# First layer norm at the end of a group's first half, column tails in one chunk, norm sums on GpSimd, query norm as the exponential's scale

## The chip, the cores and the metric

The kernel runs on one core of one Trainium2 chip. The metric is the device time of one execution in microseconds (us); less is better. The engines of a core work side by side, each through its own queue in order: TensorE (PE, with its weight loads shown as PEld), VectorE (DVE), ScalarE (ACT), GpSimd (POOL) and SyncE (SP), which here only issues transfers. Matmul results land in PSUM banks[...].

## What is computed

Everything is float32. There are 32 sequences of 256 tokens with 256 features. A conditioning attention with 16 heads of 16 features comes first, and then two layers of local attention (8 heads of 64 features, windows of 128 tokens that look at themselves and the window before) and a gated feed-forward with 682 hidden columns. What the change touches is in the layer:

```python
q = l2norm(q) * qs
k = l2norm(k) * ksc
q, k = rotary_xpos(q, k)
o = local_attention(q, k, v)
...
x = x + o @ wo
h = shift_token(x)
mu = h.mean(-1, keepdims=True)
var = h.var(-1, keepdims=True)
h = (h - mu) / jnp.sqrt(var + 1e-05) * lg + lb
h = h @ w1 + b1
a, g = jnp.split(h, 2, axis=-1)
h = a * jax.nn.gelu(g, approximate=False)
x = x + h @ w2 + b2
```

`shift_token` takes the upper half of the features from the token before. The local attention is a softmax over masked scores of q (times 8) and k.

## The kernel before

**Groups and lanes.** Two sequences form a group (G = 2), 16 groups in all. The stream of a group stands transposed in SBUF, features on partitions: `res[:, c, b, 1 + s]` holds feature half c of sequence b. The first column is zero, so the shifted input is a view that starts one column earlier for c = 1. The work of a group is cut into two lanes written as Python generators. `front(p)` (L829) holds, for both sequences, `largest` (maxima of the conditioning scores, L404 to L417), `attended` (their exponentials and weighed sums, L441 to L496), `conditioned`, and then `attention(0)`. `back(p)` (L844) holds `feedforward(0)`, `attention(1)`, `feedforward(1)`, `finish` (output) and `prepare(p + 2)` (the transposes and projections that `largest` of a later group needs). Stage p weaves `front(p)` with `back(p - 1)`. Stage 0 has a front only, and after stage 15 comes one with a back only.

**The order.** Each generator yields before a unit of work, with its kind (THIN or DENSE), a cost in us of TensorE and a delay that has to pass before it may run. `woven` (L859) runs a plan in Python: it takes the lane that is behind, in proportion to the totals FRONT and BACK (L856), and prefers a dense unit when lately there were mostly thin ones. These numbers choose only the order in which instructions are written down. The tile framework then adds the waits, and places instructions of each engine by its own estimate, so that an engine's final order may differ a little from the text.

**The feed-forward** (L714) begins with the layer norm. Two matmuls (one for each feature half) with a 128x128 tile of 1/256, `mean_w`, give the mean of every token on all partitions (L720). VectorE subtracts it (L723), ScalarE squares (L726), and eight matmuls with one column each sum the squares over the features (L732). VectorE adds the epsilon (L740), GpSimd raises to -0.5 (L741), four transposes spread the result over the partitions (L745), and VectorE writes the normalised tile `hl` (L750). The bias `lb` is folded into `b1` at the start (L270). The 682 hidden columns are NJ = 6 chunks of 128, the last with 42 columns. Each chunk of the gate and each of the value is two matmuls with 512 moving columns (L759). Gates go through GELU on ScalarE (L775), values are added and multiplied on VectorE (L783). After three chunks of each, the product with `w2` (L791) is added to the stream.

**The attention** (L514). `projections(t)` for four tiles of 128 tokens makes q, k and v (L535). For q and k, ScalarE squares (L546), VectorE sums over each head (L547) and multiplies with the rotary factors (L550, L555), and GpSimd adds the two rotary parts (L561). At the end GpSimd raises the 16 sums to -0.5 in one instruction (L564) and multiplies q and k by them (L571). `turns` transposes q and k (L586). Then eight items (two heads of one sequence) pass three steps, each a step behind the other. `scores` makes two score tiles (L599), masks them and takes the negative maxima (L614), takes exponentials (L626) and normalises (L639). `turned` transposes the weights (L647) and copies them out of PSUM. `weighed` multiplies by v (L662). `summed` applies the output projection (L676) and adds to the stream (L683). `evacuate` (L111) sends its copies in turn to VectorE (L114) and ScalarE (L116).

**Buffers.** PSUM has four banks `sc`, three `mm` and one `av`. SBUF tiles come from pools: `sb2` (12 buffers of 2 KB), `sb4` (13 of 4 KB), `sb15` (8), and small ones.

## Time and profile before

| what | value |
|---|---|
| time, median of 3 runs | 4487.06 us (4482.97 to 4487.80) |
| the profiled execution: time, span | 4488.3 us, 4486.5 us |
| mean granted TensorE clock | 0.925 |
| L759, feed-forward chunks | 1536 records, 746.8 us busy |
| L535, projections to q, k, v | 1536 records, 720.1 us |
| L732, one-column sums of squares | 512 records, 90.8 us |
| L720, means | 128 records, 66.5 us |
| L626, exponentials of the local attention | 1024, 453.3 us |
| L564, power over 128x16 on GpSimd | 128, mean 2935 ns |
| L741, power over 128x4 on GpSimd | 32, mean 1007 ns |
| L561 and L571, 128x512 on GpSimd | 256 each, mean 1270 and 1055 ns |

A float32 matmul shows as two records on TensorE. Busy times of TensorE are modelled, and records overlap, so the price of one matmul is best read from a long row of equal ones: the time from the first to the last, divided by their number. "Clock" is the share of full TensorE speed that was granted. A busy engine at half clock looks as busy as one at full clock, so both columns have to be read together. A line of a wait names the waiting instruction first, and then the one that released it.

### The profile page before, as it was taken

The numbers are of one execution on the slowest core, as the hardware profiler recorded it, in microseconds if no ns is written. First come the engines' busy times: TensorE is split into PE (matmuls) and PEld (weight loads), VectorE is DVE, ScalarE is ACT, GpSimd is POOL, SyncE is SP. The second block draws the span as 40 slices with busy tenths as digits, with TensorE's granted clock in tenths as the row PEclk, the third lists the DMA queues.
The fourth block names the chain that finished last, engine by engine and source line by source line (L and its number), as shares of the span: only waits on it lengthen the run. The fifth ranks groups of instructions, "written<-read, shape, count | busy, mean of one in ns | idle before, by whom it ended". The sixth has DMA issues, their size and how long they took to land. (4 is left out here: it accounts for less than half of the span.)

```text
span 4486.5 us, 58044 instructions
## 1 busy us (share of the span) xinstructions
PE 4288.5 (96%) x21176; PEld 2460.0 (55%) x21176; DVE 2322.7 (52%) x6679; ACT 1656.2 (37%) x4202; POOL 1079.7 (24%) x840
## 2 busy tenths in 40 slices
PE   7999999999999999999999999999999999999998
PEld 6555645555465555645556455554655556455544
DVE  2347455474644636446374454745447364463734
ACT  0334243342433424244242443424334243342423
POOL 0305040140502305032050411405023050320502
PEclk6889899898998989999898998989989899898999
DMA  3000000000000000000000000000000000000000
GB/s 122 10 1 15 15 11 15 6 15 15 15 15 1 15 15 15 15 1 15 15 15 15 11 13 8 15 15 10 19 2 15 15 15 15 2 15 15 6 5 10
DMA packets 73451, 65.53 MB, mean 15 GB/s; under 512 B 18012, under 2 KB 72016, under 8 KB 73168
## 3 DMA queue, kind: packets, MB, share of 16 engines
q1 hardware_dynamic: 64464, 53.45, 4.3%
q10 hardware_dynamic: 8704, 8.39, 0.5%
q8 instruction: 168, 2.75, 0.3%
q14 instruction: 115, 0.94, 0.1%
HBM read 35.58 MB, written 8.39 MB: 10 GB/s over the span
## 5 line engine op out<-in xcount | busy, mean ns | idle before, releaser
L759 PE MATMUL mm<-t,w 128*128 128x512 f32 (+1 forms) x1536 | 746.8, 628 | 1.7 <-DVE t L750 1.7
L535 PE MATMUL mm<-wqkv,stream 128*128 128x512 f32 x1536 | 720.1, 603 | 0.0
L626 ACT ACTIVATE e<-e,nmf 128x128 f32<-128x128 f32 (+1 forms) x1024 | 453.3, 444 | 407.9 <-DVE nmf L614 407.9
L759 PEld LDWEIGHTS mm<-t,w 128*128 128x128 f32 (+1 forms) x1536 | 269.4, 187 | 388.0 <-issue 368.2
L741 POOL TENSOR_TENSOR rstd<-rstd,minus_half 128x4 f32<-128x4 f32 x32 | 32.2, 1007 | 1832.9 <-DVE rstd L740 1832.9
L561 POOL TENSOR_TENSOR t<-t,t 128x512 f32<-128x512 f32 x256 | 324.3, 1270 | 601.4 <-DVE t L555 574.7
L783 DVE SCALAR_TENSOR_TENSOR t<-mm,b,t 128x512 f32<-128x512 f32 x192 | 143.9, 750 | 565.5 <-PE mm L759 556.4
L535 PEld LDWEIGHTS mm<-wqkv,stream 128*128 128x128 f32 x1536 | 270.8, 190 | 287.4 <-issue 255.3
L404 PE MATMUL sc<-kh,qh 17*128 17x256 f32 x2048 | 372.8, 591 | 11.9 <-DVE mx L412 11.4
L412 DVE TENSOR_REDUCE mx<-sc 128x2 f32<-128x512 f32 x512 | 320.1, 685 | 118.3 <-PE sc L404 117.1
L564 POOL TENSOR_TENSOR ss<-ss,minus_half 128x16 f32<-128x16 f32 x128 | 374.4, 2935 | 4.9
L614 DVE CUSTOM_DVE_ANT_0 e<-sc,misc 128x128 f32<-128x128 f32 (+1 forms) x1024 | 305.1, 351 | 132.9 <-PE sc L599 100.4
L791 PE MATMUL mm<-t,w 128*128 128x512 f32 (+1 forms) x768 | 368.8, 613 | 0.0
L647 PE MATMUL sc<-misc,e 128*128 128x128 f32 x1536 | 269.9, 298 | 86.0 <-DVE e L639 41.6
L451 ACT ACTIVATE t<-sc 128x512 f32<-128x512 f32 x512 | 268.4, 600 | 207.2 <-PE sc L441 133.7
L404 PEld LDWEIGHTS sc<-kh,qh 17*128 17x128 f32 x2048 | 254.4, 268 | 114.1 <-DVE mx L412 72.4
L662 PE MATMUL av<-e,t 128*64 128x256 f32 (+1 forms) x2048 | 306.7, 352 | 0.0
L639 DVE TENSOR_SCALAR e<-e,denf 128x128 f32<-128x128 f32 (+1 forms) x1024 | 292.2, 348 | 3.5
L599 PE MATMUL sc<-t,t 64*128 64x128 f32 (+1 forms) x2048 | 280.5, 365 | 12.9 <-DVE t L114 7.5
L647 PEld LDWEIGHTS sc<-misc,e 128*128 128x128 f32 x1536 | 182.7, 148 | 199.6 <-DVE nmf L614 69.1
L547 DVE TENSOR_REDUCE ss<-t 128x8 f32<-128x512 f32 x256 | 173.5, 678 | 181.0 <-ACT t L546 180.7
L571 POOL TENSOR_TENSOR t<-t,ss 128x512 f32<-128x512 f32 x256 | 264.3, 1055 | 7.7
(109 smaller groups left out, 5555.6 us busy)
## 6 DMA issues: line engine op xcount, KB each, us to landing
t<-in_x_dram SPq DMA_DIRECT2D x64, 256.0 KB
t<-in_fside_BxSxS_dram SPq DMA_DIRECT2D x32, 256.0 KB
qh<-t SPq DMA_DIRECT2D x256, 32.0 KB
kh<-t SPq DMA_DIRECT2D x256, 32.0 KB
out_dram<-t ACTq DMA_DIRECT2D x32, 256.0 KB
wqkv<-in_L_ffn_wqkv_dram SPq DMA_DIRECT2D x2, 1536.0 KB
w<-in_L_ffn_w_dram SPq DMA_DIRECT2D x2, 1364.0 KB
kh<-behind SPq DMA_DIRECT2D x128, 4.0 KB
```

Of the source, the lines that this page charges most:

```text
L404: nc.tensor.matmul(sc[i][:, t, :], lhsT=qh[r : r + CD + 1, b, g, t * P : (t + 1) * P], rhs=kh[r : r + CD + 1, b, g, :], start=True, stop=True,
L412: nc.vector.tensor_reduce(mx[:, :, 4 * g + i], sc[i], AX.X, ALU.max)
L535: nc.tensor.matmul(pm, lhsT=shifted(c, t), rhs=wqkv[l][:, c, j * INNER : (j + 1) * INNER], start=(c == 0), stop=(c == 1),)
L561: nc.gpsimd.tensor_tensor(raw[:, j], raw[:, j], rot, ALU.add)
L564: nc.gpsimd.tensor_tensor(ss.rearrange("p j h -> p (j h)"), ss.rearrange("p j h -> p (j h)"), minus_half, ALU.pow,)
L614: nc.vector.tensor_tensor_reduce(out=flat, in0=sc[i][:, w * P : (2 * w + 1) * P], in1=mask[:, w * P : (2 * w + 1) * P], scale=-1.0, scalar ...
L626: nc.scalar.activation(flat, flat, AF.Exp, bias=nm[:, i, w : w + 1], scale=-1.0, accum_out=den[:, i, w : w + 1],)
L639: nc.vector.tensor_scalar(flat, flat, den[:, i, w : w + 1], None, ALU.mult)
L647: nc.tensor.transpose(pt[:, k, :], e[:, k, :], ident)
L662: nc.tensor.matmul(acc[r : r + FD, w], lhsT=v[b][:, tile_, 2 * c + i, :], rhs=eTs[i][:, k, :].rearrange("p k q -> p (k q)"), start=start, ...
L759: nc.tensor.matmul(pm[:m, :], lhsT=w1[l][:, c, e0 : e0 + m], rhs=hl[:, c, :], start=(c == 0), stop=(c == 1),)
L791: nc.tensor.matmul(y.rearrange("p b s -> p (b s)"), lhsT=w2[l][:m, j, e * P : (e + 1) * P], rhs=acts[j - j0][:m, :], start=(j == j0), stop ...
```

## The change

- The layer norm becomes a generator of its own, `normed`. The first one runs at the end of `front(p)`, and its result is kept until `feedforward(0)` in `back(p)`, one stage later. The second stays ahead of `feedforward(1)`.
- In the norm, GpSimd adds the two shifted halves before the mean, which then is one matmul, and adds the two squared halves, so that the sums of squares are four matmuls.
- The 42 last columns of the gate and of the value stand in one chunk of weights, `w1t`: the value's at columns 0 to 41, the gate's from column 64. `w1t` is filled by GpSimd at the start, and the biases are laid out to match.
- In the local attention the query isn't scaled by its norm. The factor, `rq`, is the exponential's scale instead, and one small VectorE operation makes the bias from the four maxima of an item. So all four maxima come before the first exponential.
- GpSimd's power over 16 sums becomes two powers over 8.
- The copies of the transposed weights all go to ScalarE.
- The row tile in `largest` comes from `sb2`, the constants for iota no longer stay in SBUF, and FRONT, BACK and the units' costs and delays have other numbers.

```diff
-    minus_half = const.tile([P, 2 * FH], F32, name="minus_half")
+    minus_half = const.tile([P, FH], F32, name="minus_half")
...
-                if HID > full * P:
-                    ld(
-                        t[0 : HID - full * P, i, full : full + 1],
-                        v[full * P : HID].rearrange("(p c) -> p c", c=1),
-                    )
+                ld(
+                    t[i * FD : i * FD + HID - full * P, 0, full : full + 1],
+                    v[full * P : HID].rearrange("(p c) -> p c", c=1),
+                )
...
+        t = const.tile([P, 2, P], F32, name=f"w1t{l}")
+        nc.gpsimd.memset(t, 0.0)
+        for i in range(2):
+            nc.gpsimd.tensor_copy(
+                t[:, :, i * FD : i * FD + HID - full * P],
+                w1[l][:, :, i * HID + full * P : (i + 1) * HID],
+            )
+        w1t.append(t)
...
-        rows = sm([CH, S], "rows", 1)
+        rows = sb2([CH, S])
...
+                rq[b] = sm([P, 2, FH], "rq")
...
             nc.vector.tensor_scalar(ss, ss, 1e-24, None, ALU.max)
+            nc.gpsimd.tensor_tensor(ss[:, 1, :], ss[:, 1, :], minus_half, ALU.pow)
             nc.gpsimd.tensor_tensor(
-                ss.rearrange("p j h -> p (j h)"),
-                ss.rearrange("p j h -> p (j h)"),
-                minus_half,
-                ALU.pow,
-            )
-            for j in range(2):
-                nc.gpsimd.tensor_tensor(
-                    raw[:, j],
-                    raw[:, j],
-                    ss[:, j, :].unsqueeze(2).to_broadcast([P, FH, FD]),
-                    ALU.mult,
-                )
+                raw[:, 1],
+                raw[:, 1],
+                ss[:, 1, :].unsqueeze(2).to_broadcast([P, FH, FD]),
+                ALU.mult,
+            )
+            nc.gpsimd.tensor_tensor(rq[b][:, w, :], ss[:, 0, :], minus_half, ALU.pow)
...
                     nc.vector.tensor_tensor_reduce(
-                        out=flat,
+                        out=e[:, w : 2 * w + 1, :].rearrange("p k q -> p (k q)"),
                         in0=sc[i][:, w * P : (2 * w + 1) * P],
                         in1=mask[:, w * P : (2 * w + 1) * P],
-                        scale=-1.0,
-                        scalar=3.0e38,
+                        scale=1.0,
+                        scalar=-3.0e38,
                         op0=ALU.add,
-                        op1=ALU.min,
-                        accum_out=nm[:, i, w : w + 1],
-                    )
+                        op1=ALU.max,
+                        accum_out=nm[:, w, i : i + 1],
+                    )
+                es.append(e)
+            scale = rq[b][:, :, 2 * c : 2 * c + 2]
+            nc.vector.scalar_tensor_tensor(nm, nm, -1.0, scale, ALU.mult, ALU.mult)
+            for i in range(2):
                 for w in range(2):
-                    flat = e[:, w : 2 * w + 1, :].rearrange("p k q -> p (k q)")
+                    flat = es[i][:, w : 2 * w + 1, :].rearrange("p k q -> p (k q)")
                     nc.scalar.activation(
                         flat,
                         flat,
                         AF.Exp,
-                        bias=nm[:, i, w : w + 1],
-                        scale=-1.0,
+                        bias=nm[:, w, i : i + 1],
+                        scale=scale[:, w, i : i + 1],
                         accum_out=den[:, i, w : w + 1],
                     )
-                es.append(e)
...
-                evacuate(eT, pt)
+                nc.scalar.copy(eT, pt)
...
-    def feedforward(l, res):
-
+    def normed(l, res, to):
         shifted = [res[:, c, :, 1 - c : 1 - c + S] for c in range(2)]
-        yield DENSE, 1.72, 1.5
+
+        xs, cen = sb2([P, G, S]), sb4([P, 2, T])
+        nc.gpsimd.tensor_tensor(xs, shifted[0], shifted[1], ALU.add)
+        yield DENSE, 0.86, 3.5
         pm = bank("mm", (P, G, S))
-        for c in range(2):
-            nc.tensor.matmul(pm, lhsT=mean_w, rhs=shifted[c], start=(c == 0), stop=(c == 1))
-        cen, sq = sb4([P, 2, T]), sb4([P, 2, T])
+        nc.tensor.matmul(
+            pm.rearrange("p b s -> p (b s)"), lhsT=mean_w, rhs=xs.rearrange("p b s -> p (b s)"),
+            start=True, stop=True,
+        )
+        sq = sb4([P, 2, T])
         for c in range(2):
             nc.vector.tensor_tensor(
                 cen[:, c, :].rearrange("p (b s) -> p b s", b=G), shifted[c], pm, ALU.subtract
             )
             nc.scalar.activation(sq[:, c], cen[:, c], AF.Square)
-
-        yield THIN, 2.0, 3.5
+        nc.gpsimd.tensor_tensor(sq[:, 0], sq[:, 0], sq[:, 1], ALU.add)
+
+        yield THIN, 1.0, 5.0
         pv = bank("mm", (P, NT))
         for t in range(NT):
-            for c in range(2):
-                nc.tensor.matmul(
-                    pv[:, t : t + 1],
-                    lhsT=sq[:, c, t * P : (t + 1) * P],
-                    rhs=mean_w[:, 0:1],
-                    start=(c == 0),
-                    stop=(c == 1),
-                )
+            nc.tensor.matmul(
+                pv[:, t : t + 1],
+                lhsT=sq[:, 0, t * P : (t + 1) * P],
+                rhs=mean_w[:, 0:1],
+                start=True,
+                stop=True,
+            )
         rstd = sm([P, NT], "rstd", 2)
         nc.vector.tensor_scalar(rstd, pv, 1e-5, None, ALU.add)
         nc.gpsimd.tensor_tensor(rstd, rstd, minus_half[:, 0:NT], ALU.pow)
...
-        hl = sb4([P, 2, T])
+        hl = to[l] = sb4([P, 2, T])
         for c in range(2):
             nc.vector.scalar_tensor_tensor(
                 hl[:, c, :], cen[:, c, :], lg[l][:, c : c + 1], pr, ALU.mult, ALU.mult
             )
 
-        def half(i, j):
-            m = min(P, HID - j * P)
+    def feedforward(l, res, of):
+
+        hl = of.pop(l)
+
+        def hidden(w):
             pm = bank("mm")
             for c in range(2):
-                e0 = i * HID + j * P
                 nc.tensor.matmul(
-                    pm[:m, :],
-                    lhsT=w1[l][:, c, e0 : e0 + m],
-                    rhs=hl[:, c, :],
-                    start=(c == 0),
-                    stop=(c == 1),
+                    pm, lhsT=w[:, c, :], rhs=hl[:, c, :], start=(c == 0), stop=(c == 1)
                 )
-            return m, pm
-
-        run = NJ // 2
-        for j0 in range(0, NJ, run):
+            return pm
+
+        def gate(pm, bias, m=P):
+            act = sb2([P, T])
+            nc.scalar.activation(act[:m, :], pm, AF.Gelu, bias=bias)
+            return act
+
+        def gated(act, pm, bias, m=P):
+            nc.vector.scalar_tensor_tensor(
+                act[:m, :], pm, bias, act[:m, :], ALU.add, ALU.mult
+            )
+
+        last = HID - full * P
+        for js in (range(0, 3), range(3, full)):
             acts = []
-            for j in range(j0, j0 + run):
+            for j in js:
                 yield DENSE, 1.72, 0.0 if j else 2.5
-                m, pm = half(1, j)
-                act = sb2([P, T])
-                nc.scalar.activation(
-                    act[:m, :], pm[:m, :], AF.Gelu, bias=b1[l][:m, 1, j : j + 1]
+                e0 = HID + j * P
+                acts.append(
+                    (P, j, gate(hidden(w1[l][:, :, e0 : e0 + P]), b1[l][:, 1, j : j + 1]))
                 )
-                acts.append(act)
-            for j in range(j0, j0 + run):
+            if js[-1] == full - 1:
+
                 yield DENSE, 1.72, 0.0
-                m, pm = half(0, j)
-                act = acts[j - j0]
-                nc.vector.scalar_tensor_tensor(
-                    act[:m, :], pm[:m, :], b1[l][:m, 0, j : j + 1], act[:m, :], ALU.add, ALU.mult
-                )
+                pm, bias = hidden(w1t[l]), b1[l][:, 0, full : full + 1]
+                act = gate(pm[FD : FD + last, :], bias[FD : FD + last, :], last)
+                gated(act, pm[0:last, :], bias[0:last, :], last)
+                acts.append((last, full, act))
+            for m, j, act in acts:
+                if m == P:
+                    yield DENSE, 1.72, 0.0
+                    gated(act, hidden(w1[l][:, :, j * P : (j + 1) * P]), b1[l][:, 0, j : j + 1])
             for e in range(2):
-                yield DENSE, 2.58, 0.0 if e else 1.5
+                yield DENSE, 0.86 * len(acts), 0.0 if e else 1.5
                 y = bank("mm", (P, G, S))
-                for j in range(j0, j0 + run):
-                    m = min(P, HID - j * P)
+                for n, (m, j, act) in enumerate(acts):
                     nc.tensor.matmul(
                         y.rearrange("p b s -> p (b s)"),
                         lhsT=w2[l][:m, j, e * P : (e + 1) * P],
-                        rhs=acts[j - j0][:m, :],
-                        start=(j == j0),
-                        stop=(j == j0 + run - 1),
+                        rhs=act[:m, :],
+                        start=(n == 0),
+                        stop=(n == len(acts) - 1),
                     )
                 part = res[:, e, :, 1:]
-                if j0:
+                if js[0]:
                     nc.vector.tensor_tensor(part, part, y, ALU.add)
...
         yield from attention(0, res, last if p else chain(last, prepare(1)) if NG > 1 else last)
+        yield from normed(0, res, kept[p])
 
     def back(p):
 
         res = stream[p % 2]
-        yield from feedforward(0, res)
+        yield from feedforward(0, res, kept[p])
         yield from attention(1, res, ())
         for n in range(G * (p + 2), min(G * (p + 3), B)):
             loaded[n] = load_sequence(n)
-        yield from feedforward(1, res)
+        yield from normed(1, res, kept[p])
+        yield from feedforward(1, res, kept[p])
         yield from finish(p, res)
         if p + 2 < NG:
             yield from prepare(p + 2)
 
-    FRONT, BACK, LEAD, SHARE, MEMORY = 85.0, 142.0, 0.08, 0.5, 3.0
+    FRONT, BACK, LEAD, SHARE, MEMORY = 88.0, 135.0, 0.08, 0.5, 3.0
```

## The prediction

> **What bounds the kernel now.** I read the engine sums and slices first, then the chain, the groups of instructions, the clock by windows, TensorE's timeline of one stage, and last the order of the instructions on each engine in the two built programs.
>
> The page of the kernel before, engine sums and two slice rows:
>
> ```profile
> PE 4288.5 (96%) x21176; PEld 2460.0 (55%) x21176; DVE 2322.7 (52%) x6679; ACT 1656.2 (37%) x4202; POOL 1079.7 (24%) x840
> ...
> PE   7999999999999999999999999999999999999998
> ...
> PEclk6889899898998989999898998989989899898999
> ```
>
> TensorE is busy for 96% of the span and no other engine for more than 52%, so work taken off TensorE counts in full wherever it is dense. The chain of waits followed back from the end covers only the last 6% or so, the drain, and says little of the stages. The clock row dips regularly. Windows of 3.41 us (the columns are busy us of TensorE, its weight loads, VectorE, ScalarE, GpSimd, then the granted clock) show where:
>
> ```profile
> 2162.02:2165.43 3.41, 2.74 (x20) 1.44 (x19) 3.41 (x7) 1.86 (x3) 0.00 (x0) 1.00 0.00 0
> 2165.43:2168.84 3.41, 3.41 (x20) 2.38 (x20) 3.21 (x6) 0.65 (x1) 0.00 (x0) 0.77 0.00 0
> 2168.84:2172.25 3.41, 3.41 (x19) 2.56 (x17) 2.08 (x4) 0.00 (x0) 0.00 (x0) 0.50 0.01 2
> ...
> 2189.30:2192.71 3.41, 3.41 (x8) 1.35 (x5) 2.08 (x4) 0.81 (x2) 0.25 (x1) 0.50 0.00 0
> 2192.71:2196.12 3.41, 3.41 (x9) 1.40 (x8) 0.00 (x0) 1.45 (x3) 0.00 (x0) 0.73 0.00 0
> ```
>
> For some 27 us at the start of a stage (one front and one back woven together) TensorE has half its clock. Its timeline there, start and length first:
>
> ```profile
> 2159.28 1.15 PE L404 MATMUL sc<-kh,qh 17*128 17x256 f32 x16
> 2160.35 1.99 PE L720 MATMUL mm<-stream,mean_w 128*128 128x512 f32 x4
> 2162.27 1.84 PE L404 MATMUL sc<-kh,qh 17*128 17x256 f32 x16
> 2164.77 6.55 PE L404 MATMUL sc<-kh,qh 17*128 17x256 f32 x32 [0.67 <-DVE mx L412]
> 2171.26 3.57 PE L732 MATMUL mm<-mean_w,t 128*128 128x1 f32 x16
> 2175.27 0.59 PE L421 MATMUL sc<-misc,nm 128*16 128x128 f32 x2 [0.44 <-DVE nm L414]
> 2175.79 6.72 PE L404 MATMUL sc<-kh,qh 17*128 17x256 f32 x32
> 2182.44 1.11 PE L745 MATMUL mm<-misc,rstd 128*128 128x128 f32 x4
> 2183.48 6.72 PE L404 MATMUL sc<-kh,qh 17*128 17x256 f32 x32
> 2190.13 5.89 PE L759 MATMUL mm<-t,w 128*128 128x512 f32 x8
> ```
>
> The front runs `largest` (L404, thin, paced by the maxima on VectorE) while the back runs the first layer norm, a chain of small steps. Neither has dense matmuls, the clock falls, and the first feed-forward chunk (L759) itself runs at half speed. Two records are one matmul, so eight at full clock would be 3.4 us. Stages repeat every 273.0 us (the next first L404 stands at 2432.30), 15 times.
>
> **The skill.** "TensorE: Matmul & The Clock Gate", section "What's actually happening", says that the array's clock is halved after about one idle window of 3.4 us and restored after a busy one. The trace agrees on 0.50 and on windows of 3.4 us, but here the fall came beside busy, thin matmuls, some 6 us after the last dense one. The same page, "Architectural detail", says that ScalarE, VectorE and GpSimd are strict FIFOs, so whatever stands behind a waiting instruction waits too; I use that below. "ScalarE: Activation LUTs", "What ACT_TABLE_LOAD costs", puts a load at 1283 ns; the trace has 1283 ns. It adds a drain, which I don't use.
>
> **The change, part by part.** Prices: a 512-column matmul 0.858 us (24 records of L759 in 10.30 us); a thin group L404 1.07 us (start to start, 2159.28 to 2160.35); a one-column matmul 0.246 us (14 records of L732 in 1.72 us).
>
> 1. *TensorE work removed.* Per feed-forward, the tails in one chunk save 2 matmuls (1.72 us), the mean from a presummed tile one (0.86), the variance 4 one-column matmuls (0.98): 3.56 us. There are two in a stage, 7.1 us, and 32 in all, 114 us. All are on TensorE's own queue, the bound.
>
> 2. *Start of a stage.* Before, from the first L404 at 2159.28 to the second L421's end at 2196.2 is 36.9 us. At full clock and without waits its content is 8 L404 groups 8.6, L720 1.9, L732 2.0, L745 0.6, L421 0.6, six matmuls of L759 5.15: 18.9 us. So 18.0 us are lost. In the new order the same stretch holds, beside the eight thin groups, half the variance, the broadcast, 16 chunk matmuls and 6 of the second product: 8.6+1.0+0.6+0.7+13.7+5.2 = 29.8 us. VectorE needs 32 maxima at 0.685 (21.9) and some 6 us more, so TensorE stays the longer. Waits worked through in order: 0.9 us for the squares' sum on GpSimd, 1.2 for the power (1.01 us), 0.2 for the normalised tile, 1.9, 1.2 and 0.7 for banks that the maxima free: 5.7-6 us. The clock is unknown: between the last dense matmul of the front's preparation and the first chunk lie some 6 us, enough for one or two windows at half clock; I take 2 us. Loss 8 instead of 18: 10 us gained. Bounds: 14 if the clock holds and the waits overlap, 5 if it falls as long as before. Moving the norm itself to the stage's end costs nothing on its first leg: between the residual add (L683) and the mean stand over 7 us of preparation matmuls, against 0.69 (add) + 1.27 (sum on GpSimd, price of L561) us.
>
> 3. *The second layer norm, mid-stage.* Here the GpSimd sums cost. In the new order the sum of the two halves stands on GpSimd behind a whole projection: rotary add 1.27, power for k, power for q, scaling 1.05. A power over 128x4 takes 1.007 us and over 128x16 2.935, so over 128x8 I take 1.65, on the line between them. From the end of the last k projection: squares, reduction and rotary products 2.9 us, then 1.27+1.65+1.65+1.05+1.27 = 6.9, so the mean may start after 9.9 us. TensorE has only 8 output-projection matmuls, 2 for v and 4 scores till then, 6.3 us: it waits 3.7. VectorE has the centring queued ahead of the next maxima's scaling, so it waits as well and the exponentials start late: centring 0.7, a square 0.6, four exponentials 2.5, reciprocal and scaling 0.6 before the next transposes, against 0.95 of scores: 3.9 us more. The later transposes and chunks then wait 0.6 and 1.3. Sum 9.5, less the 0.4 us idle there before: 9. Bounds: 3 (the power is cheaper, the waits absorb later ones) and 13 (two clock windows on top). The pattern stands alike in every stage's order.
>
> 4. *Scores.* Each exponential now needs all four maxima and one small product: two maxima pairs later, about 1.4-0.4+0.2 = 1.2 us longer to the first transposes. In the order of one stage, before, three places have under 4.5 us of TensorE work between scores and transposes; the trace waits 2.35 and 2.03 us in two of them. After there are as many outside the norm: +2 us. The copies of the transposed weights all go to ScalarE: 256 more at 0.467 = 120 us of ScalarE, 256 at 0.549 = 141 us off VectorE, which is 80-99% busy where two attentions overlap. Table loads rise from 121 to 153 by the alternation of exponentials and GELUs in the orders, 41 us of ScalarE, hidden below 66% busy. Bounds -2 (VectorE's relief wins) and +5; I take +2.
>
> 5. *One answer each.* Query scaling off GpSimd: 128 x 1.03 = 132 us less, powers +0.37 x 128 = 47 more, two sums x 32 x 1.27 = 81 more: even. Weights of the tail chunk, copied once on GpSimd beside weight loads that TensorE waits for anyway (17.8 us at L270): under 1 us, and if that cover goes, under 2. Smaller constants, another buffer for `rows`: nothing; no wait over 0.3 us on it before.
>
> 6. *Sum.* Per stage -7.1 -10 +9 +2 = -6.1, times 15 = -92. First and last stage: two feed-forwards less 7, layer norms standing alone 2 dearer: -5. The profiled execution took 4488.3 us (span 4486.5), 1 above the median 4487.06: 4488.3-97 = 4391, so 4390 against the median.
>
> **Rivals.**
> - *The sums are hidden* (GpSimd is ahead of TensorE mid-stage). For it: GpSimd is only 24% busy, and TensorE waited 3.9 us in all for its scalings. Against: the queue counted in part 3. Without the 9 us: -15.1 x 15 - 5 = -232, 4255.
> - *The half clock moves to mid-stage* (slower). The two waits of 3.7 and 3.9 us lie 2 us apart with only scores between. If the clock falls there and stays, each us of it costs half. It decides from 6.1 us of lost clock, 12.2 us at 0.50 per stage. At 20 us, +3.9 x 15 - 5 = +54: 4540; at the 27 us that the stage start showed, about 4595. Against: dense chunks follow within 10 us, and the two-window dip at 2282-2290 healed at once.
> - *ScalarE and the longer score chain eat the gain.* ScalarE at 66% in 2310-2320 leaves little for two more copies per pair. At +6 instead of +2 with a start gain of 8: -7.1-8+9+6 = 0 per stage, and with the ends 4482.
>
> **How the numbers follow.** Forecast 0.66, hidden sums 0.12, moved half clock 0.15, score chain 0.07. The forecast's own range, from bounds of 4.5, 5 and 3.5 us per stage that won't fall together, is 4310 to 4475. Half of the first rival lies below 4260 and most of the second above 4500, so 4260 to 4500 leaves out about 2 in 10. About 0.2% (9 us) is what a measurement of this kernel can tell: slower 0.17 (second rival, a part of the third), same 0.05, faster 0.78.
>
> **What would show it.** Right: granted clock near 1.0 at the stage starts with L404's successor alternating with chunks; three 512-column and four one-column matmuls fewer in each feed-forward with its norm; a TensorE wait of 3-4 us on GpSimd before each mid-stage mean, followed by one on the weights' scaling. Wrong: half clock still at the start, or no wait at the mean, or 12 us and more at half clock after it.

## The result, and the profile after

The changed kernel takes 4593.25 us, median of 4 runs (4591.79 to 4595.05), against 4486.02 us for the kernel before: a ratio of 1.024, 95% interval 1.0222 to 1.0258. The forecast was 4390, the range 4260 to 4500. The direction was wrong. The profiled execution took 4592.3 us, its span 4590.5, 104 more than before.

The page of the changed kernel, engine sums and two slice rows:

```profile
PE 4233.5 (92%) x20720; PEld 2362.5 (51%) x20720; DVE 2214.5 (48%) x6679; ACT 1881.8 (41%) x4490; POOL 1065.8 (23%) x910
...
PE   7998999989999998999989999899999999999897
...
PEclk8798999889998999899989998899988998899899
```

TensorE has 456 records fewer, and yet its row now has eights where it had nines: it waits. Summed over the view of waits, its idle time went from 186.6 to 347.6 us (59.0 of it put down to "issue", of which more below). The lost clock (the sum of 1 minus the granted clock over windows of 2 us) went from 336 to 441 us. A stage takes 280.0 us, not 273.0, and 15 times 7.0 is 105, about the 104.

*The start of a stage.* Windows of 3.41 us and TensorE's timeline there, in the columns of the prediction:

```profile
2209.41:2212.82 3.41, 3.18 (x20) 2.55 (x19) 0.94 (x4) 0.05 (x1) 1.59 (x2) 0.80 0.24 49
2212.82:2216.23 3.41, 3.20 (x16) 1.89 (x14) 1.52 (x3) 0.00 (x0) 0.69 (x1) 0.50 0.04 9
...
2223.05:2226.46 3.41, 3.41 (x18) 2.05 (x16) 1.87 (x4) 1.97 (x2) 0.00 (x0) 0.50 0.01 2
2226.46:2229.87 3.41, 3.41 (x21) 1.23 (x19) 0.77 (x2) 0.69 (x1) 0.00 (x0) 0.70 0.00 0
2229.87:2233.28 3.41, 3.41 (x12) 1.51 (x9) 2.68 (x5) 1.38 (x2) 0.25 (x1) 1.00 0.00 0
```

```profile
2209.93 0.70 PE L409 MATMUL sc<-kh,qh 17*128 17x256 f32 x4
2210.86 1.35 PE L738 MATMUL mm<-mean_w,t 128*128 128x1 f32 x8 [0.23 <-POOL t L733]
...
2216.61 2.08 PE L767 MATMUL mm<-t,w 128*128 128x512 f32 x2
2218.61 2.09 PE L409 MATMUL sc<-kh,qh 17*128 17x256 f32 x16
2220.63 2.08 PE L767 MATMUL mm<-t,w 128*128 128x512 f32 x2
...
2251.42 0.38 PE L426 MATMUL sc<-misc,nm 128*16 128x128 f32 x2
```

The weave is the one read from the order: thin groups alternate with chunks. But the clock still falls, for 17 us instead of 27, and a single chunk matmul (two records) takes 2.08 us in it. From the first L409 to the second L426's end (2251.8) is 41.9 us for a content of 29.8: 12.1 us lost, where the prediction had 8.

*One whole stage*, 2209.9 to 2489.9 us, the largest waits of TensorE (us in total, times, longest):

```profile
PE sc L649 <- DVE e L641: 8.8, 3, 5.8
PE sc L446 <- issue: 3.9, 1, 3.9
PE mm L723 <- POOL t L720: 3.3, 1, 3.3
PE mm L767 <- DVE t L756: 1.2, 1, 1.2
```

The third and fourth were foreseen: the second layer norm's mean waits for the sum on GpSimd. The first two, except 3.0 us of L649 that lie beside the same norm, lie elsewhere and come from the conditioning attention. GpSimd's timeline there:

```profile
2286.94 0.62 POOL L501 TENSOR_TENSOR t<-t,den 128x256 f32<-128x256 f32 x1
2287.52 1.64 POOL L570 TENSOR_TENSOR ss<-ss,minus_half 128x8 f32<-128x8 f32 x1
2289.14 1.63 POOL L577 TENSOR_TENSOR rq<-ss,minus_half 128x8 f32<-128x8 f32 x1
2290.74 0.62 POOL L494 TENSOR_TENSOR t<-t,es 128x256 f32<-128x256 f32 x1
```

VectorE and TensorE in the same microseconds:

```profile
2287.12 0.25 DVE L492 RECIPROCAL den<-den 128x16 f32<-128x16 f32 x1
2291.39 0.42 DVE L500 TENSOR_TENSOR t<-t,sc 128x256 f32<-128x256 f32 x1 [4.01 <-POOL t L494]
```

```profile
2287.27 0.71 PE L446 MATMUL sc<-qh,kh 18*128 18x256 f32 x6
2291.91 2.04 PE L446 MATMUL sc<-qh,kh 18*128 18x256 f32 x10 [3.93 <-issue]
```

L494 is the attention's own-value product, a small 128x256 multiplication on GpSimd that the change doesn't touch. It stands behind the powers of the other lane's projection. In the kernel before, at the same place, the product (there L489) stands ahead of the power:

```profile
2265.47 0.61 POOL L489 TENSOR_TENSOR t<-t,es 128x256 f32<-128x256 f32 x1
2266.40 1.26 POOL L561 TENSOR_TENSOR t<-t,t 128x512 f32<-128x512 f32 x1 [0.32 <-DVE t L555]
2267.62 0.62 POOL L496 TENSOR_TENSOR t<-t,den 128x256 f32<-128x256 f32 x1
2268.20 2.91 POOL L564 TENSOR_TENSOR ss<-ss,minus_half 128x16 f32<-128x16 f32 x1
```

L500 on VectorE adds it to a transposed tile in a score bank and so frees the bank. VectorE stands for 4.01 us, and TensorE resumes 0.1 us after L500 has ended. "Issue" names no engine, so the cause was tested. The same delay comes again 34 us later, there with VectorE's scaling of the local attention queued behind L500. TensorE's timeline:

```profile
2318.86 1.15 PE L600 MATMUL sc<-t,t 64*128 64x128 f32 x8
2325.80 1.16 PE L649 MATMUL sc<-misc,e 128*128 128x128 f32 x4 [5.79 <-DVE e L641]
```

Within each gap the clock halves (3.4 and 5.1 us lost). Before, VectorE's same addition (L495) held TensorE up by 1.3 us a stage.

*The second norm, mid-stage*, in another stage:

```profile
2113.61 2.07 PE L723 MATMUL mm<-t,mean_w 128*128 128x512 f32 x2 [3.30 <-POOL t L720]
2115.61 1.65 PE L600 MATMUL sc<-t,t 64*128 64x128 f32 x8
2119.78 0.95 PE L649 MATMUL sc<-misc,e 128*128 128x128 f32 x3 [2.52 <-DVE e L641]
```

GpSimd's timeline ahead of this mean is the queue that the prediction worked through:

```profile
2108.25 1.65 POOL L570 TENSOR_TENSOR ss<-ss,minus_half 128x8 f32<-128x8 f32 x1
2109.87 1.64 POOL L577 TENSOR_TENSOR rq<-ss,minus_half 128x8 f32<-128x8 f32 x1
2111.47 1.04 POOL L571 TENSOR_TENSOR t<-t,ss 128x512 f32<-128x512 f32 x1
2112.47 1.09 POOL L720 TENSOR_TENSOR t<-stream 128x512 f32<-128x512 f32 x1
```

The mean, 1.02 us long at the end of a front (2206.46), takes 2.07 here. From 2112 to 2130 the granted clock was 0.53: 8.5 us lost, where the kernel before loses none beside this norm.

### The profile page after: what moved, and what is told of

Read it like the earlier page. It is cut to its first block, busy times and chain, and to the rows that moved or that the text cites. A ratio compares the mean times of both kernels' runs of the same rounds, so it can differ in the third digit from the quotient of the medians.

```text
span 4590.5 us, 58091 instructions
## 1 busy us (share of the span) xinstructions
PE 4233.5 (92%) x20720; PEld 2362.5 (51%) x20720; DVE 2214.5 (48%) x6679; ACT 1881.8 (41%) x4490; POOL 1065.8 (23%) x910
## 4 chain that ended last, share of the span: by engine, by line
PE 81%; DVE 6%; issue 6%; POOL 4%; ACT 2%; DMA 0%; SPq 0%; POOLq 0%; DVEq 0%; ACTq 0%
PE mm L767 15%; PE mm L541 13%; PE mm L806 8%; PE av L664 6%; PE mm L301 5%; PE sc L649 5%; PE sc L446 5%; PE sc L409 5%; PE sc L600 4%; PE mm L678 3%; PE av L464 3%; PE sc L587 3%; PE mm L367 2%; POOL ss L570 1%; ACT e L629 1%
## 5 line engine op out<-in xcount | busy, mean ns | idle before, releaser
L541 PE MATMUL mm<-wqkv,stream 128*128 128x512 f32 x1536 | 763.6, 623 | 0.0
L767 PE MATMUL mm<-t,w 128*128 128x512 f32 x1280 | 664.6, 652 | 19.3 <-DVE t L756 19.3
L629 ACT ACTIVATE e<-e,nmf,rq 128x128 f32<-128x128 f32 (+1 forms) x1024 | 546.7, 536 | 294.0 <-DVE nmf L625 293.8
L649 PE MATMUL sc<-misc,e 128*128 128x128 f32 x1536 | 293.9, 320 | 146.1 <-DVE e L641 143.9
L767 PEld LDWEIGHTS mm<-t,w 128*128 128x128 f32 x1280 | 237.2, 203 | 282.0 <-issue 234.9
L806 PE MATMUL mm<-t,w 128*128 128x512 f32 (+1 forms) x768 | 372.1, 613 | 0.0
L649 PEld LDWEIGHTS sc<-misc,e 128*128 128x128 f32 x1536 | 199.3, 158 | 320.9 <-DVE e L641 182.4
L552 ACT ACTIVATE t<-mm 128x512 f32<-128x512 f32 x256 | 153.4, 599 | 454.7 <-PE mm L541 454.7
L651 ACT COPY e<-sc 128x384 f32<-128x384 f32 x512 | 227.8, 477 | 273.1 <-PE sc L649 272.1
L720 POOL TENSOR_TENSOR t<-stream 128x512 f32<-128x512 f32 x32 | 34.8, 1089 | 1157.7 <-DVE stream L685 1079.9
L446 PE MATMUL sc<-qh,kh 18*128 18x256 f32 x2048 | 242.6, 447 | 61.8 <-issue 59.0
L774 ACT ACTIVATE t<-mm,b 128x512 f32<-128x512 f32 x192 | 132.2, 688 | 386.2 <-PE mm L767 384.7
```

The source lines that it names most:

```text
L446: nc.tensor.matmul(sc[i][:, k, :], lhsT=kh[r : r + CD + 2, b, g, k * P : (k + 1) * P], rhs=qh[r : r + CD + 2, b, g, :], start=True, stop=True,
L541: nc.tensor.matmul(pm, lhsT=shifted(c, t), rhs=wqkv[l][:, c, j * INNER : (j + 1) * INNER], start=(c == 0), stop=(c == 1),)
L629: nc.scalar.activation(flat, flat, AF.Exp, bias=nm[:, w, i : i + 1], scale=scale[:, w, i : i + 1], accum_out=den[:, i, w : w + 1],)
L649: nc.tensor.transpose(pt[:, k, :], e[:, k, :], ident)
L767: nc.tensor.matmul(pm, lhsT=w[:, c, :], rhs=hl[:, c, :], start=(c == 0), stop=(c == 1))
L806: nc.tensor.matmul(y.rearrange("p b s -> p (b s)"), lhsT=w2[l][:m, j, e * P : (e + 1) * P], rhs=act[:m, :], start=(n == 0), stop=(n == len ...
```

## The experiments

Four theories: A, the norms' sums on GpSimd and the half clock they bring; B, the attention product in GpSimd's queue; C, the place of the first norm itself; D, the score chain with the query's scale in the exponential. Times are medians, ratios are to the kernel before measured beside it, with 95% intervals. What is "gained" or "lost" is a difference of medians. Where an edit needs it, the units' costs and delays (e1, e5) or the lanes' totals (e3, e10, e12, e16) change with it.

**Undoing one part of the change.** *e1_no_sums*: the sums back on TensorE, two matmuls for the mean and eight with one column for the squares (all else as after).

```diff
-        nc.gpsimd.tensor_tensor(xs, shifted[0], shifted[1], ALU.add)
...
+        for c in range(2):
+            nc.tensor.matmul(pm, lhsT=mean_w, rhs=shifted[c], start=(c == 0), stop=(c == 1))
```

> The changed kernel with the norm's sums back on TensorE: the mean is two matmuls, the sums of squares eight, nothing of the norm but the power is left on GpSimd. Theory A (the sums on GpSimd, mid-stage): the waits of 3.3, 3.0 and 1.2 us at the second norm and most of its 8.5 us of lost clock go, 3.7 us of matmuls per stage come back: -9 x 15, 4450 to 4470 us. Theory B (GpSimd's queue delays the conditioning attention's products, and these the banks and the weights): only the wait of 3.3 us goes and 3.7 us come back: 4580 to 4600. Theory C (the place of the first norm shifts the lanes against each other): 4580 to 4600.

4539.69 us, ratio 1.0116 (1.0093 to 1.014): 54 us gained on the changed kernel. A is real, but about half of what was lost, and it is not the half clock that went: TensorE's waits fell from 347.6 to 261.2 us, while the lost clock over the run stayed (441 and 444 us). At the second norm 5.1 us of it are lost instead of 8.5, but as much is lost elsewhere in the stage.

*e2_query_scaled*: one power over 128x16, queries multiplied on GpSimd, the score chain as before.

```diff
-            nc.vector.scalar_tensor_tensor(nm, nm, -1.0, scale, ALU.mult, ALU.mult)
-                        scale=scale[:, w, i : i + 1],
+                        scale=-1.0,
```

> The changed kernel with the query scaled on GpSimd as before: one power over 16 sums, two scalings, exponentials with a fixed scale and one maximum each. Theory D (longer chain from scores to weights, four exponentials 0.36 us dearer per item): each of the three waits on the scaled weights shortens by 1.2 us, ScalarE has 92 us less: 4530 to 4550. Theories A and B: GpSimd's block of powers and scalings is as long as before (5.0 us against 4.3), so no gain: 4585 to 4615.

4534.36 us, 1.0096 (1.0074 to 1.0118): 59 gained. VectorE's wait for the attention's product (L500 for L494) did not fall in it, 136.0 us against 117.9, so this gain does not come from B.

*e3_norm_in_back*: the first norm at the start of the back half again.

```diff
     def front(p):
...
-        yield from normed(0, res, kept[p])
     def back(p):
...
+        yield from normed(0, res, kept[p])
...
-    FRONT, BACK, LEAD, SHARE, MEMORY = 88.0, 135.0, 0.08, 0.5, 3.0
+    FRONT, BACK, LEAD, SHARE, MEMORY = 85.6, 137.4, 0.08, 0.5, 3.0
```

> The changed kernel with the first norm at the start of the back lane again (totals of the lanes corrected by the norm's 2.4). Theories A and B: the half clock at the stage start comes back to 27 us and the stage start loses the 6 us it had gained: 4660 to 4690. Theory C: the order in the rest of the stage goes back to that of the kernel before, and the removed matmuls show: 4400 to 4480.

4486.94 us, 0.9996 (0.9988 to 1.0005): 106 gained, although the start of a stage lost 15.4 to 17.1 us of clock again (8.5 with the change). VectorE's wait for the product fell from 117.9 to 23.0 us over the run, and TensorE's wait for the sum (L723 for L720), still on GpSimd, from 54.9 to 3.1. So the place of the first norm (with the lanes' totals that go with it), which shifts the two lanes against each other, brings both the product and the second norm's sum behind the powers: A and B share this cause.

*e4_tv_vector*: L494 alone, from GpSimd to VectorE.

```diff
-            nc.gpsimd.tensor_tensor(
+            nc.vector.tensor_tensor(
                 tv,
```

> The changed kernel with one product of the conditioning attention (own value times own weight, L494, 64 in all at 0.62 us) on VectorE instead of GpSimd. Theory B: the waits of 3.9 and 5.8 us on TensorE fall to about 1 and 2.5 and the half clock after them (8.5 us lost per stage) mostly goes: 4430 to 4480. Theories A, C and D: VectorE carries 27 us more and nothing else changes: 4580 to 4600.

4467.34 us, 0.9949 (0.9932 to 0.9966): 126 gained by one word. Its waits over the whole run:

```profile
PE sc L649 <- DVE e L641: 103.1, 64, 6.2
PE mm L723 <- POOL t L720: 55.0, 18, 3.3
...
PE sc L446 <- issue: 9.2, 15, 0.6
```

The "issue" wait was 59.0 us and is 9.2; the score chain's was 143.9 and is 103.1; the sum's wait is untouched. The lost clock fell from 441 to 387 us. Waits and clock give 85 + 55 = 140 for a span that fell by 127; the two overlap.

**Pairs, and the kernel before.** *e5_tv_no_sums* is e4 with the sums of e1; *e6_tv_sums_vector* is e4 with both sums on VectorE (`nc.vector.tensor_tensor` in the two places).

> The changed kernel with the attention's product on VectorE and the norm's sums back on TensorE. Theory B alone being the cost: the sums give back 3.7 us of matmuls per stage and nothing else: 4500 to 4525. Theory A as a second cost beside B: the wait of 3.3 us for the mean, those of 3.0 and 1.2 after it and most of the 8.5 us of lost clock there go as well: 4370 to 4430.

> The changed kernel with the product and both sums of the norm on VectorE, so that TensorE keeps the fewer matmuls. Theory A as a second cost: like the run with the sums on TensorE but 3.7 us per stage less: 4320 to 4390. Rival (the wait comes from the norm's place in the order, not from GpSimd): the mean waits for VectorE's queue instead and the half clock stays: 4450 to 4480.

4398.23 us (0.9808, 0.979 to 0.9827) and 4382.70 us (0.9767, 0.9751 to 0.9782). Off GpSimd the sums gain 69 or 85 us more. TensorE's wait for the mean's input, 55.0 us over the run in e4, is 1.6 and 3.9. At the second norm 5.1 us of clock are lost in both, against 6.8 to 8.5 in most stages of e4. VectorE carries the sums better than TensorE.

*e7_before_tv*: the kernel before with the same product on VectorE.

> The kernel before with the same one product on VectorE. If its delay was there before the change, the 126 us are no part of the change's cost: 4370 to 4400. If the change made it (two powers ahead of it in a new order), only the wait of 1.3 us per stage goes: 4455 to 4490.

4484.43 us, 0.9993 (0.9984 to 1.0002). Where it was, the product cost no time that can be told from zero; the change made it late.

*e8_before_tails*: the kernel before with the tails in one chunk alone (with the smaller constants and the buffer for `rows` that make room for it).

```diff
+        for i, j, w in chunks + [(0, full, w1t[l])]:
+                act = gate(pm[FD : FD + last, :], bias[FD : FD + last, :], last)
+                gated(act, pm[0:last, :], bias[0:last, :], last)
```

> The kernel before with the column tails in one chunk, and with the smaller constants and the row tile from the larger pool, which make room for its weights. All theories: two matmuls of 0.858 us fewer in each of 32 feed-forwards, on the bound: 4487 - 55 = 4432, 4420 to 4445; if the order shifts as in theory C, anything from 4400 to 4500.

4431.98 us, 0.9878 (0.9863 to 0.9894): 55.5 us gained. The prediction's two matmuls of 0.86 us in 32 feed-forwards are 55.0.

**With A and B gone.** Three edits of e6 (4382.7 us): *e9_all* adds the edit of e2, *e10_fixed_back* the edit of e3, and *e11_fixed_turn* copies the transposed weights in turn again (`evacuate(eT, pt)` for `nc.scalar.copy(eT, pt)`).

> The kernel after with the attention product and both norm sums on VectorE (4382.7 us), and in addition the queries scaled on GpSimd as before, with one power over 128x16 and a fixed scale in the exponentials. On the kernel after, this undoing gained 59 us. Theory B (that gain was the shorter delay of the attention product behind the powers in GpSimd's queue, which no longer carries the product): nothing is left to gain, 4375 to 4400 us. Theory D (the exponential with a scale tile and the longer score chain cost of themselves): the 93 us of ScalarE time come back and the score chain is shorter, some 4300 to 4350 us. Third: the query's scale as the exponential's is worth what it takes from GpSimd, and undoing it makes 4400 to 4450 us.

> The same 4382.7 us kernel, but with the first norm at the start of a group's back half again (lane lengths 85.6 and 137.4). On the kernel after this undoing gained 106 us. If the place at the end of the front is worth what step 2 of the prediction finally showed at the stage's start (6 us a stage), undoing it costs about 90 us: 4460 to 4490 us. Theory C (the place as such costs, by moving attention work against the norm and GpSimd's queue): undoing it gains again, 4290 to 4350 us. If it only matters together with the two GpSimd delays, within 20 us: 4365 to 4405 us.

> The same 4382.7 us kernel, but with the copies of the transposed exponentials taken in turn by VectorE and ScalarE as before. TensorE waits 107 us in this kernel at the transposes for the normalised exponentials, which VectorE writes. If the move to ScalarE is what holds that chain up (ScalarE now has the dearer exponentials and all the copies), 4300 to 4350 us. If it relieves VectorE, which has the product and the sums too here, undoing it costs: 4400 to 4450 us. If neither, within 20 us.

e9: 4249.55 us, 0.9465 (0.9441 to 0.9488), 133 gained, more than any theory had said. e10: 4491.61 us, 1.0006 (0.9995 to 1.0017), 109 lost: the first norm's new place is a gain once the two GpSimd delays are gone. e11: 4341.02 us, 0.9669 (0.9647 to 0.9691), 42 gained. The page of e9:

```profile
PE 4081.5 (96%) x20720; PEld 2289.2 (54%) x20720; DVE 2275.0 (53%) x6551; ACT 1793.1 (42%) x4490; POOL 1045.9 (25%) x782
...
PEclk8799999999999999999999999999999999999999
```

TensorE is busy for 96% again, with the smaller number of records, and no slice after the start-up is under 90% of the clock. At the second norm 1.7 us of clock are lost in every other stage and none in the rest (e6: 5.1), at the start of a stage 8.5 as in the changed kernel.

**Inside the query's scale, and the parts that were meant to gain.** e9 differs from e6 in three things, so two were put back one at a time. *e14_two_powers*: two powers over 128x8. *e15_scale_tile*: the exponential's minus one from a tile.

```diff
-                        scale=-1.0,
+                        scale=minus_one,
```

*e12_two_parts_alone* is the kernel before with the tails and the first norm's place alone. *e13_all_turn* is e9 with the copies in turn.

> The kernel before with two parts of the change alone, the tails in one chunk and the first norm at the end of the front (lane lengths as after); sums on TensorE, queries scaled on GpSimd, copies in turn, and the attention product on GpSimd. If steps 1 and 2 hold as sized by the runs (tails 55 us, place 106 to 109 us), 4315 to 4335 us. If the product on GpSimd is late without the second power and the sums too (theory B, not bound to them), waits as after and over 4400 us. If the place of the first norm gains only in company of the other edits, 4425 to 4440 us.

> The kernel with product and sums on VectorE and queries scaled on GpSimd (4249.6 us), and in addition the transposed exponentials' copies in turn by VectorE and ScalarE. If the copies on ScalarE cost by themselves, the 42 us that the turn gained in the 4382.7 us kernel come again: 4200 to 4215 us. If they only cost beside the dearer exponentials on ScalarE, 4240 to 4260 us.

> The same 4249.6 us kernel with the power of the keys' and queries' sums in two pieces of 128x8 (about 1.65 us each for one of 2.94), keys first, all else the same. If the two powers are what the 133 us were, 4350 to 4385 us. If the exponential or the chain is, 4245 to 4265 us.

> The same 4249.6 us kernel with the exponential's fixed scale of minus one given as a tile of 128x1 that holds minus one: 90 ns more in each of 1024 exponentials, all else the same. If the dearer exponentials are what the 133 us were, 4340 to 4385 us. If it is the order of the score chain, 4250 to 4270 us.

e14: 4262.68 us (0.9488, 0.9442 to 0.9534; its runs lie between 4238 and 4281): its interval covers e9. In its trace TensorE's order is e9's, record for record, so the two powers as such cost little or nothing. e15: 4319.38 us (0.9629, 0.9615 to 0.9644), 70 lost, between the two ranges expected. ScalarE's groups of exponentials in e9, and then in e15:

```profile
L631 ACT ACTIVATE e<-e,nmf 128x128 f32<-128x128 f32 (+1 forms) x1024 | 455.5, 446 | 374.0 <-DVE nmf L619 368.9 <-DVE denf L640 4.0 <-DVE e L644 0.5
```

```profile
L633 ACT ACTIVATE e<-e,nmf,minus_one 128x128 f32<-128x128 f32 (+1 forms) x1024 | 548.3, 536 | 391.2 <-DVE nmf L621 386.6 <-DVE denf L642 1.9 <-ACT e L656 0.2
```

An exponential with a scale tile takes 90 ns more (536 for 446). The engine is busy for only 42% of the span, but four exponentials stand in the chain between a score and its transpose.

e13: 4282.09 us (0.9545, 0.9531 to 0.956), 33 us slower than e9, in neither range expected, where the same edit had gained 42 on e6. The copies' place has no sign of its own. e12: 4523.88 us (1.0083, 1.0068 to 1.0098), slower than before with nothing but the two parts that were counted as gains. VectorE waits in e12:

```profile
DVE t L500 <- POOL t L494: 132.2, 46, 4.6
```

With the tails alone (e8) that wait is 34.7 us, as it was in the kernel before (34.7, L495 for L489). So B needs neither the sums nor the split power; the first norm's place is enough.

*e16_two_parts_vector* is e12 with the edit of e4. *e17_score_order* is e9 with the changed order of the score chain alone put back. All four maxima of two heads come first, then one small product on VectorE, then the four exponentials, where e9 has two maxima and their two exponentials for each head:

```diff
-                        accum_out=nm[:, i, w : w + 1],
+                        accum_out=nm[:, w, i : i + 1],
...
+            nc.vector.tensor_scalar(nm, nm, -1.0, None, ALU.mult)
+            for i in range(2):
...
-                        scale=-1.0,
+                        scale=1.0,
```

> The kernel of 4524 us (tails in one chunk and first norm at the end of the front, all else as before) with the attention product on VectorE. If the product's place behind the powers is what spoiled the two parts, what their steps came to in the runs is left, 55 and about 107 us: 4310 to 4345 us. If something else of the first norm's place costs, little changes: 4450 to 4520 us.

> The kernel of 4249.6 us (product and sums on VectorE, queries scaled on GpSimd, fixed scale) with the changed order of the score chain alone: all four maxima of a pair of heads, one small VectorE multiplication of them, then the four exponentials with a fixed scale. If the order makes the rest of the 133 us, 4300 to 4330 us; if the scale tile and the order only cost together, 4250 to 4270 us; below 4245 us the order gains of itself.

e16: 4387.08 us, 0.9774 (0.9757 to 0.979), 137 gained by the product's move, but short of the 4310 to 4345 expected. e17: 4359.99 us, 0.9711 (0.9696 to 0.9725), 110 lost by this edit alone, more than the 50 to 80 expected. The scale tile and the order by themselves lose 70 and 110, together more than the 133 between e6 and e9, so the two prices overlap. One and the same place in a stage, on ScalarE and TensorE, first in e9:

```profile
2157.43 0.40 ACT L631 ACTIVATE e<-e,nmf 128x128 f32<-128x128 f32 x1 [1.78 <-DVE nmf L619]
```

```profile
2157.22 1.49 PE L604 MATMUL sc<-t,t 64*128 64x128 f32 x8
2160.65 0.47 PE L652 MATMUL sc<-misc,e 128*128 128x128 f32 x1 [1.94 <-DVE e L644]
```

and then in e17:

```profile
2211.05 0.40 ACT L632 ACTIVATE e<-e,nmf 128x128 f32<-128x128 f32 x1 [2.89 <-DVE nmf L628]
```

```profile
2209.74 1.49 PE L604 MATMUL sc<-t,t 64*128 64x128 f32 x8
2214.75 0.47 PE L652 MATMUL sc<-misc,e 128*128 128x128 f32 x1 [3.52 <-DVE e L644]
```

Measured from the last group of scores (L604), the first exponential starts at +0.21 us in e9 and at +1.31 in e17. The transposes wait 1.6 us longer. Over the run TensorE's waits grew by 50 us and the lost clock by 56 (247 to 303), together 106 of the 108 that the span grew. In e15 it is 18 and 41 for a span that grew by 68.

The framework places instructions by its own estimate, so most edits also move matmuls on TensorE. Compared record by record in order of time, some 390 of 20,720 stand elsewhere in e4, 780 in e15, 1,310 in e17, 1,560 between e6 and e9, and 17 of 21,176 in e7. In e15, e17 and the 133 us of e9 the price therefore contains the order that the edit brings; how much of it is order was not separated.

## Why the prediction was wrong

**Step 1 (work removed) was right.** 456 records fewer are the prediction's 7 matmuls, two records each, in 32 feed-forwards, and 8 in the start-up. The tails alone gave 55.5 us for 55.0 (e8).

**Step 2 (start of a stage) failed twice.** Its order and its 29.8 us of content were right. The clock term was mis-sized: taken as 2 us, measured as 8.5; what else was lost there, 3.6 us, is less than the 5.7 to 6 of waits. From 18.0 us lost before, that left 5.9 us a stage, not 10. The 18.0 is itself too small: it counts six chunk matmuls before the second L421's end, where the trace has four, so 19.8 us were lost and 7.7 gained (the place as a whole is worth 7.3, see below). The worse failure is "costs nothing on its first leg". That sentence looked only at the moved norm's own wait. The move also shifts the conditioning attention against the other lane's projections, so that L494 comes to stand behind the powers (e3, e12). On the changed kernel this delay is worth 126 us (e4), or 8.4 us a stage; with the two parts alone it turns a gain into 39 us of loss (e12 less the kernel before). Step 5 had GpSimd "even": right as a sum of busy time (1079.7 before, 1065.8 after), and no answer at all to who stands behind whom. The prediction had cited the Trainium skill, "TensorE: Matmul & The Clock Gate", section "Architectural detail", on strict FIFOs, and then applied it to the norm's sums only. The trace agrees for the product: L494 starts at 2290.74, as the second power (2289.14 and 1.63 long) ends. With the delays gone, the place is worth 109 us, 7.3 a stage (e10 against e6). With the sums on TensorE it is less: e16 is 45 us below e8.

**Step 3 (second norm) had its waits right.** The mean waits 3.30 us for 3.7, the transposes 2.52 and 0.52 for 3.9, the chunk 1.18 for 1.3. It had 9 us a stage and no lost clock in them. The runs give back 85 us where nothing goes to TensorE instead (e6 against e4, 5.7 a stage), and 69 us where 3.7 us a stage of matmuls return (e5, 8.3 with them). So the price was about right, though the waits were 7.5 us and not 9.5 and a part of it is lost clock, which the step left out. That the waits arise at all hangs on the first norm's place (e3).

**Step 4 (scores) had its mechanism right and its size wrong.** It worked out 1.2 us more to the transposes; the pair above shows 1.6. It then took +2 us a stage, with +5 as its bound. Undoing the query's scale gives 59 us on the changed kernel and 133 in e6: 3.9 and 8.9 us a stage. Two terms were missing. The first is the dearer exponential. The Trainium skill, "ScalarE: Activation LUTs", section "What ACT_TABLE_LOAD costs", says that each operand of one value per partition adds about 93 ns to an activation. The trace agrees with 90, and e15 puts it at 70 us with the order it brings. The second is the clock: with the longer gaps between thin scores and transposes more half clock came, so that in e17 the loss is about twice what the waits alone show (50 and 56 us). The copies, which the step also counted, decide no sign (e11, e13); the table loads rose as foreseen, from 122 to 154, stand alike in the changed kernel and in e9, and were not tested.

**Step 6 (the sum), mended.** Per stage: -7.1 for work removed, -7.3 for the place, +5.7 for the sums, +8.4 for the product, and between +3.9 and +8.9 for the score chain: +3.6 to +8.6, where 7.0 was measured. The terms don't add exactly, since a wait inside a stretch of half clock is shared by two causes.

**The rivals.** The first, hidden sums, is refuted. The second, half clock at mid-stage, happened beyond the point it named (17 us at half clock against 12.2), but alone it doesn't make the result: at 17 us it would give (8.5 - 6.1) x 15 - 5 = +31 us. That its figure for 27 us, about 4595, lies beside the 4593 measured is chance: 6.8 and 10.2 us more of half clock stand at the two gaps of the product, which it did not name. The third, the score chain, took +6 us for a term that the runs put at 3.9 to 8.9, and had the smallest chance. The product in GpSimd's queue, 126 us on the changed kernel, was in no case.

The fastest version measured is e9 (e14 can't be told from it): tails in one chunk and first norm at the end of the front kept, the product and the norm sums on VectorE, the query scaled as before. It takes 4249.55 us, 5.3% less than the kernel before (ratio 0.9465, 0.9441 to 0.9488).

## What to carry to other kernels

When a block of work moves against another lane, go through the queue of every shared engine, and not only the moved block's own waits: a 0.6 us instruction that nobody touched, put behind two powers of 1.65 us, cost 126 us here. A wait on TensorE can cost more than its length where thin work surrounds it (50 us of waits and 56 of lost clock in e17), but no fixed factor holds: in e1, 86 us of waits went and the lost clock stayed. A chain's length counts even on an engine that is idle for more than half of the time: price each added operand and each "all before the first" by how often the chain has too little matmul work beside it.

## What the hardware showed that was not expected

The half clock outlives its cause. In the stage shown first it began within gaps of 3.9 and 5.8 us and lasted some 7 and 10 us in all. At the second norm it began within the gap of 3.3 us and lasted 17 us, over a second gap of 2.5 us, among busy transposes and matmuls with few rows. The Trainium skill, "TensorE: Matmul & The Clock Gate", section "What's actually happening", has the clock restored after one busy window of some 3.4 us; here four windows in a row at the stage's start have TensorE busy for 3.41 us of 3.41 (2216.23 to 2229.87, two of them shown above) and a clock of 0.50, 0.50, 0.50 and 0.70. The power on GpSimd has a price per element and a fixed one: 1.01 us for 128x4, 1.65 for 128x8, 2.94 for 128x16.
